# Convolution sums in PSUM, a scan's first group in parts, and transposes in attention

## The chip, the cores and the metric

The kernel runs on one core of a Trainium2 chip, as one launch. The metric is the device time of a launch in microseconds (us); a median over runs is given. The engines are TensorE (PE; its weight loads are listed as PEld), VectorE (DVE), ScalarE (ACT), GpSimd (POOL) and SyncE (SP), whose queue issues the DMAs.

## The reference, cut to what matters

An image batch `x` of 2 x 56 x 56 x 128 passes through four layers, each of them a mixing part and in the last two a feed-forward part:

- Layer 0: a two-dimensional state-space scan (`ss2d`) over 256 inner channels: input projection, depthwise 3x3 convolution with bias and SiLU, four scan directions with 16 states, norm, gate, output projection.
- Layer 1: the same on four heads of 32 channels, one after the other, because each head's input is the sum of its own slice and the output of the head before:

```
for i in range(1, g):
    s = prev + chunks[i]
    prev = _vss_block(s, p) + vss_skip * s      # norm, in_proj, 3x3 conv, SiLU, 4 scans, gate, out_proj
```

- Layer 2: attention of the tokens with themselves as queries, keys and values (one head of 128 channels, 3136 tokens in each of two images), then a spectral mixer (long filters on the token axis).
- Layer 3: attention with projected queries, keys and values, then a mixture of experts.

What is computed by the convolution of one head of layer 1: with both images stacked, 128 channels (64 inner channels x 2 images) of 56 x 56 points, `row = silu(sum over 9 taps of tap * shifted(pad) + bias)`. What is computed by attention for 448 queries: `exp(scale * q.k)` over all keys, the weighted sum of V, and the division by the row sum.

## The kernel before, in words

**Tiling.** A plane of 3136 positions is worked in 7 chunks of 448 columns (`CH`, eight image rows), or in quarters of 784 (`QT`) in the scans, which are 7 tiles of 112 tokens (`TP`, `TS` = 7).

**Layer 1.** `Layer1.run` goes through the heads. It runs the scan of a head (`Scans.run`, some 616 us, an order written out by hand in `emit`), and then a stage between two scans: for each chunk c from 0 to 7, `after` finishes the head just scanned (norm, gate, output projection: L1024 to L1055) and `before` prepares the next head. `before` of chunk c adds the residual (L982), normalises, transposes the tokens to channels (`pt`, L992, copied to `hT`, L994), projects them (L996), writes the result with a border into `pad` (ACT, L997), does the convolution of chunk c - 1 (which needs one row of chunk c), and projects the gate (L1008, L1009). At c == 2 it calls `Scans.first`.

**The convolution** is `conv_rows`. By PE (L522) it is nine matmuls with a diagonal matrix for each tap, in fp32 two passes each, summed in a PSUM tile `pcv`. By DVE it is one TENSOR_SCALAR (L526) and eight SCALAR_TENSOR_TENSOR (L528), summed in place in an SBUF tile `cv`. In heads 1 to 3 the calls c = 2, 4, 5, 6 go to DVE, c = 1, 3, 7 to PE. Then ACT takes the SiLU into `row` (L529; printed as `big`) and POOL copies it into the column order `col` (L530).

**The first group of the next scan** (`Scans.first`) makes what the scan's first sixteen steps read, all at once at c == 2: `rows` (projection, L173, copied by ACT, L185), `keep` (DMA of the rows to DRAM, L189), `fetch` (back, L196), `band` and `rest` (three bf16 bands of each row: ACT L199, POOL L202), `store` (L206), `spread` (the tile `three`, L212), `steps` and `soft` (the step sizes `delta`, L221), `times` (`du`, DVE L231), `across` and `turn` (transposes on PE, L236, copied by ACT, L237). All PSUM tiles of it are `pcv`. In the scan, `spread` (PE, L407) repeats a row of `three` over the partitions into the bank pair `b`, DVE multiplies it by `du` (`h`, L479), scans (L401), POOL multiplies by `c` (L495), and PE adds up (L421).

**PSUM in a stage.** The pools are opened for a stage and closed for the scan, whose own pools take the same banks. Before: `pmid1` with two buffers each of `p`, `pv`, `pt`, and `pcon1` with two buffers of `pcv`.

**Order.** On each engine the order is that of the program; a wait on one engine holds all that is behind it. All DMAs named here are in SP's queue.

**Attention.** `Attend.run` works in 14 chunks (2 images x 7). For each of 25 key tiles PE makes the scores (L1224), ACT the exponentials (L1226), POOL the running row sum `total` (L1237), PE the weighted sum (L1218). At the end of a chunk the sum is copied to SBUF as `by`; four matmuls (L1253) bring it to tokens and apply `out_w`, which for layer 2 is the identity matrix, and four (L1256) sum `total` over the partitions. In layer 3, `Queries.some` prepares the next chunk's queries beside this: low-precision scores (L1159) and their maxima (L1163, L1166); then four matmuls with the identity (L1169) put the 4 x 112 negative maxima into one row in PSUM, ACT copies it to `shift` (L1174), and a bf16 matmul with `part` (L1176) spreads it over the partitions and DVE adds it to `q` (L1177).

Of the kernel before, what the change touches and what calls it, by code (L numbers as in the profile page):

```python
# [14 lines left out]
F32 = mybir.dt.float32  # L15
# [95 lines left out]
class Scans:  # L111
# [138 lines left out]
            soft=soft, copy=copy, times=times, across=across, turn=turn,  # L250
        )

    def first(self, pool):

        self.begin()
        own = {
            "xd": self.y[0][:, 0:QT], "whole": self.y[-1][:, QT : QT + QT // 4],
            "BT": self.y[0][:, QT + QT // 4 : QT + QT // 4 + 32 * TS],
        }
        f = self.pieces_of(self.groups[0], lambda name, n: own[name], self.dram0)  # L260

        def ps():
            return pool.tile([128, CH], F32, name="pcv").unsqueeze(1)

        for i in range(2):
            f["rows"]([i], ps())
        f["keep"]()
        f["fetch"]()
        for i in range(3):
            f["band"](i)  # L270
            if i < 2:
                f["rest"](i)
        f["store"]()
        f["spread"]()
        for ci in range(self.nch):
            for i in range(2):
                f["steps"](ci, [i], ps())
        for ci in range(self.nch):
            f["soft"](ci)
        for ci in range(self.nch):  # L280
            f["times"](ci, False)
        f["across"](ps())
        for ci in range(self.nch):
            for i in range(0, TS, 3):
                f["turn"](ci, ps(), range(i, min(i + 3, TS)))

    def preparation(self, groups, short):

# [219 lines left out]
def conv_rows(k, pools, pad, diag, taps, bias, row, col, c, by):  # L508


    nc = k.nc
    sp, pp = pools
    cs = slice(CH * c, CH * (c + 1))

    def shifted(t):
        dy, dx = divmod(t, 3)
        return pad[:, 8 * c + dy : 8 * c + dy + 8, dx : dx + HW]

    if by == "PE":
        s = pp.tile([128, CH], F32, name="pcv")  # L520
        for t in range(9):
            nc.tensor.matmul(s, lhsT=diag[:, t, :], rhs=shifted(t), start=t == 0, stop=t == 8)  # L522
    else:
        s = sp.tile([128, CH], F32, name="cv")
        v = s.rearrange("p (r w) -> p r w", w=HW)
        nc.vector.tensor_scalar(v, shifted(0), taps[:, 0:1], None, ALU.mult)  # L526
        for t in range(1, 9):
            nc.vector.scalar_tensor_tensor(v, shifted(t), taps[:, t : t + 1], v, ALU.mult, ALU.add)  # L528
# [92 lines left out]
def layer0(k, d, big, follow):  # L621
# [3 lines left out]
    with ExitStack() as ctx:  # L625
# [46 lines left out]
        with ExitStack() as sctx:  # L672
# [117 lines left out]
            for b in range(B):  # L790
                with ExitStack() as bctx:
                    sp = bctx.enter_context(k.pool(f"mid{b}", 2))
                    pp = bctx.enter_context(k.pool(f"pmid{b}", psum=True))
                    cp = bctx.enter_context(k.pool(f"pcon{b}", 2, psum=True))
                    ip = bctx.enter_context(k.pool(f"pads{b}"))
                    if b > 0:
                        outs = outputs(ip)
                    pads = []
                    diag = ip.tile([128, 9, 128], F32, name="diag")
                    for ci in range(2):  # L800
                        pads.append(ip.tile([128, PAD, PAD], F32, name=f"pad{ci}"))
# [12 lines left out]
                    diagonals(k, diag, W["taps"][:, 0])  # L814
                    for c in range(NCH + 1):
                        if b == 0 and c == 2:
                            norm(1, (ap, tp), groups)
                        if b > 0 and c < NCH:
                            after(b - 1, (sp, pp, ip), c, *outs)
                        before(b, (sp, cp), c, pads, diag)  # L820
                        if c == 2:
                            scans.first(cp)
                scans.run()
        with ExitStack() as bctx:
            sp = bctx.enter_context(k.pool("midl", 2))
# [10 lines left out]
class Layer1:  # L836
# [133 lines left out]
    def before(self, head, pools, c, pad):  # L970
# [30 lines left out]
        if c > 0:  # L1001
            conv_rows(
                k, (sp, vp), pad, self.diag, W["taps"], W["conv_b"], self.row, self.col, c - 1,
                "DVE" if c in ((2, 3, 4, 5, 6) if head == 0 else (2, 4, 5, 6)) else "PE",
            )
        if c < NCH:
            ps = vp.tile([128, CH], F32, name="pcv")
            nc.tensor.matmul(ps, lhsT=W["in_w"][:, 1, :], rhs=hT, start=True, stop=True)  # L1008
            nc.scalar.activation(self.z[:, cs], ps, AF.Silu, bias=self.inb[:, 1:2])  # L1009
        if c == 2:  # L1010
            self.scans.first(vp)

    def after(self, head, pools, c):

# [53 lines left out]
    def opened(self, ctx):  # L1068
        k, name = self.k, "mid1"
# [13 lines left out]
    def run(self, follow):  # L1083


        k = self.k
        for head in range(1, 5):
            self.scans.run()
            with ExitStack() as ctx:
                pp = ctx.enter_context(k.pool("pmid1", 2, psum=True))  # L1090
                if head < 4:
                    pad = self.opened(ctx)
                    sp = self.sp
                else:
                    sp = ctx.enter_context(k.pool("mid1", 2))
                    chunk = follow(ctx)
                for c in range(NCH + 1):
                    if c < NCH:
                        self.after(head - 1, (sp, pp), c)
                    if head < 4:  # L1100
                        self.before(head, (sp, pp, self.vp), c, pad)
                    elif c < NCH:
                        self.last(sp, c)
                        chunk(c)
# [18 lines left out]
class Queries:  # L1123
# [27 lines left out]
    def some(self, left):  # L1151
# [12 lines left out]
        if not self.todo:  # L1164
            m = self.sp.tile([TP, 4], F32, name="mm")
            nc.vector.tensor_reduce(m, self.m, AX.X, ALU.max, negate=True)  # L1166
            ps = self.banks("pr")
            for i in range(4):
                nc.tensor.matmul(  # L1169
                    ps[0:1, TP * i : TP * (i + 1)], lhsT=m[:, i : i + 1], rhs=self.k.ident[:TP, :TP],  # L1170
                    start=True, stop=True,
                )
            row = self.sp.tile([1, CH], BF16, name="shift")
            nc.scalar.copy(row, ps[0:1, 0:CH])  # L1174
            ps = self.banks("pr")[:, 0:CH]
            nc.tensor.matmul(ps, lhsT=self.part, rhs=row, start=True, stop=True)  # L1176
            nc.vector.tensor_tensor(self.q, self.q, ps, ALU.add)  # L1177
# [6 lines left out]
class Attend:  # L1184
# [18 lines left out]
    def run(self, keys, queries, V, scale, out_w, skip=None, also=lambda at, j: None):  # L1203
# [4 lines left out]
        for at, (b, qc) in enumerate(chunks):  # L1208
# [41 lines left out]
            pt = four(self.bank("pr"))  # L1250
            pd = av[:TP, CH : CH + 4]
            for i in range(4):
                nc.tensor.matmul(  # L1253
                    pt[:, i, :], lhsT=by[:, TP * i : TP * (i + 1)], rhs=out_w, start=True, stop=True
                )
                nc.tensor.matmul(  # L1256
                    pd[:, i : i + 1], lhsT=total[:, TP * i : TP * (i + 1)], rhs=self.ones, start=True, stop=True
                )
# [7 lines left out]
class Attention2:  # L1266
# [30 lines left out]
    def run(self, early, inputs):  # L1297
# [3 lines left out]
        with k.pool("a2") as sp, ExitStack() as ctx:  # L1301
# [923 lines left out]
```

## Time and profile before

| what | value |
|---|---|
| median of 3 runs | 8746.86 us (8737.68 to 8752.10) |
| profiled execution, its own time | 8761.79 us |
| its span | 8760.0 us |
| mean granted TensorE clock | 0.964 |
| PE, DVE, ACT, POOL busy | 91%, 76%, 64%, 78% |
| scans of layer 1 (start to end, us) | 2768.6 to 3384.7, 3483.9 to 4101.5, 4200.6 to 4814.6, 4912.2 to 5528.4 |
| gaps between them | 99.2, 99.1, 97.6 us |
| a chunk of layer 2's attention | 43.3 us |
| a chunk of layer 3's attention | 54.5 us (early), 49.2 us (later) |

A row of the timeline or of a group reads: start in the span (or the line), busy time, engine, line, operation, output and inputs by the program's names, shapes, and count. In brackets stands how long the engine was idle before and on what it waited. In a windows row, the stretch and its length are followed by the busy time of each engine with its number of instructions, the granted clock of PE as a share of full speed, the share of the DMA engines that was busy, and GB/s. The profiled execution took 14.9 us more than the median of the runs.

### The profile page before, as it was taken

Reading aid. Unit: us, or ns where it says so; the run is one execution under the profiler, and the core shown is the slowest. Engines: PE = TensorE matmul, PEld = TensorE weight load, DVE = VectorE, ACT = ScalarE, POOL = GpSimd, SP = SyncE. Lnnn points to the kernel's source line nnn. Section 1 sums busy time; section 2 is a strip of 40 time slices with the busy share of each in tenths; the row PEclk is TensorE's granted clock in tenths of the full one; section 3 lists DMA queues with packets and bytes.
Section 4 is the critical chain, followed back from the end, with each engine's and each line's share of the span. In section 5 each row is a group of like instructions: output and inputs, shape, how many; then the busy total and the mean of one; then the engine's idle time right before and its main releaser. Section 6 shows DMA issues by size and latency. Waiting matters only on the chain. (4 is left out here: it accounts for less than half of the span.)

```text
span 8760.0 us, 106320 instructions
## 1 busy us (share of the span) xinstructions
PE 8013.3 (91%) x32199; PEld 4929.5 (56%) x32199; DVE 6642.9 (76%) x6889; ACT 5622.6 (64%) x12956; POOL 6845.1 (78%) x4232
## 2 busy tenths in 40 slices
PE   8999999999998898898888889699899989989998
PEld 4555555555555454445444455355488878865555
DVE  8999998999996997998899799711266676665442
ACT  6888876888876997998898799543322222224330
POOL 5999986999995997998899799566667767756551
PEclk9999999999998999999999999799999999989999
DMA  5666663666663884886788598300133433310004
GB/s 147 217 217 210 211 194 115 217 218 214 211 199 96 228 224 127 218 224 165 183 230 219 130 232 223 80 14 4 47 97 102 116 87 101 102 47 8 15 1 140
DMA packets 846633, 1276.86 MB, mean 146 GB/s; under 512 B 182813, under 2 KB 504350, under 8 KB 846058
## 3 DMA queue, kind: packets, MB, share of 16 engines
q1 hardware_dynamic: 846058, 1270.07, 51.8%
q8 instruction: 254, 4.16, 0.2%
q14 instruction: 321, 2.63, 0.1%
HBM read 1230.00 MB, written 46.58 MB: 146 GB/s over the span
## 5 line engine op out<-in xcount | busy, mean ns | idle before, releaser
L495 POOL TENSOR_TENSOR p<-h,c 128x784 f32<-128x784 f32 x2048 | 3765.8, 1867 | 209.2 <-DVE h L401 114.0
L401 DVE TENSOR_TENSOR_SCAN h<-a,state,h 128x784 f32<-128x784 f32 x1104 | 1993.7, 1834 | 29.5 <-POOL h L498 27.2
L421 PE MATMUL acc<-p,center 128*128 128x392 f32 x4096 | 1482.7, 500 | 24.3 <-POOL p L495 24.2
L421 PE MATMUL acc<-p,ident 128*128 128x392 f32 x4096 | 1427.8, 492 | 0.5 <-POOL p L495 0.4
L479 DVE TENSOR_TENSOR h<-du,b 128x784 f32<-128x784 f32 x1024 | 976.9, 954 | 192.5 <-PE b L407 175.5
L421 PEld LDWEIGHTS acc<-p,center 128*128 128x128 f32 x4096 | 747.6, 192 | 546.6 <-POOL p L495 57.2
L421 PEld LDWEIGHTS acc<-p,ident 128*128 128x128 f32 x4096 | 746.5, 190 | 532.4 <-issue 29.5
L1237 POOL TENSOR_TENSOR total<-total,e 128x448 f32<-128x448 f32 (+1 forms) x644 | 735.6, 1142 | 328.7 <-ACT e L1226 289.4
L1226 ACT ACTIVATE e<-sc 128x448 f32<-128x448 f32 (+1 forms) x700 | 377.5, 543 | 723.2 <-PE sc L1224 594.6
L498 POOL TENSOR_TENSOR h<-du,b 128x784 f32<-128x784 f32 x448 | 832.8, 1859 | 0.0
L381 ACT ACTIVATE a<-delta,L1A 128x784 f32<-128x784 f32 x768 | 700.9, 913 | 148.3 <-DVE h L401 144.2
L401 DVE TENSOR_TENSOR_SCAN h<-h,state,a 128x784 f32<-128x784 f32 x432 | 795.4, 1841 | 0.0
L381 ACT ACTIVATE a<-delta,L0A 128x784 f32<-128x784 f32 x704 | 643.0, 914 | 169.8 <-DVE h L401 164.4
L359 ACT ACTIVATE X<-X,BT 112x128 f32<-112x128 f32 x2100 | 683.7, 390 | 0.2
L401 DVE TENSOR_TENSOR_SCAN h<-a,h 128x784 f32<-128x784 f32 x368 | 644.3, 1775 | 29.5 <-POOL h L498 24.0
L1741 POOL TENSOR_TENSOR u<-u,T 128x1024 f32<-128x1024 f32 x192 | 448.9, 2359 | 264.8 <-DVE u L1739 264.8
L407 PE MATMUL b<-three,sel 96*128 96x512 bf16 (+1 forms) x2048 | 516.1, 333 | 100.2 <-DVE h L479 42.7
L1725 ACT ACTIVATE less<-cv 128x512 f32<-128x512 f32 x256 | 152.2, 595 | 611.5 <-PE cv L1703 586.2
L359 ACT ACTIVATE big<-big,BT 112x64 f32<-112x64 f32 x1680 | 446.4, 336 | 0.0
L359 ACT ACTIVATE pair<-big,BT 112x64 f32<-112x64 f32 x1680 | 444.0, 337 | 0.0
L1737 ACT ACTIVATE T<-T 128x1024 f32<-128x1024 f32 x128 | 135.2, 1056 | 407.5 <-DVE T L1735 279.0
L407 PEld LDWEIGHTS <-sel 96*128 96x128 bf16 x2048 | 198.1, 100 | 319.9 <-issue 214.1
(545 smaller groups left out, 15050.5 us busy)
## 6 DMA issues: line engine op xcount, KB each, us to landing
c<-rows SPq DMA_DIRECT2D x1024, 392.0 KB, 4.0
c<-rows SPq DMA_DIRECT2D x2048, 196.0 KB, 4.6
b<-rows SPq DMA_DIRECT2D x512, 196.0 KB, 4.7
b<-rows SPq DMA_DIRECT2D x192, 392.0 KB, 4.5
wA<-win SPq DMA_DIRECT2D x64, 448.0 KB, 3.9
wB<-win SPq DMA_DIRECT2D x64, 448.0 KB, 6.3
wC<-win SPq DMA_DIRECT2D x64, 448.0 KB, 4.8
wD<-win SPq DMA_DIRECT2D x64, 448.0 KB, 3.8
```

Of the source, the lines that this page charges most:

```text
L359: self.k.nc.scalar.activation(x["bT"][:, i, c0:c1], g["duT"][x["ci"]][:, i, c0:c1], AF.Copy, scale=g["BT"][:, r : r + 1])
L381: self.k.nc.scalar.activation(x["a"], g["delta"][ci], AF.Exp, scale=self.w["A"](g["kd"], ci, x["n"]))
L401: self.k.nc.vector.tensor_tensor_scan(h, a, b, start, ALU.mult, ALU.add)
L407: self.k.nc.tensor.matmul(ps[:, c0:c1], lhsT=self.w["selB"](x["n"]), rhs=x["g"]["three"][:, c0:c1], start=True, stop=True)
L421: nc.tensor.matmul(job["acc"][:, i, 0:392], lhsT=self.w["sum"], rhs=x["p"][:, 392 * i : 392 * (i + 1)], start=False, stop=n == NS - 1,)
L479: nc.vector.tensor_tensor(one["h"], one["g"]["du"][one["ci"]], one["b"], ALU.mult)
L495: nc.gpsimd.tensor_tensor(now["p"], now["h"], now["c"], ALU.mult)
L498: nc.gpsimd.tensor_tensor(three["h"], three["g"]["du"][three["ci"]], three["b"], ALU.mult)
L1226: nc.scalar.activation(e[:n], ps[:n], AF.Exp, scale=scale)
L1237: nc.gpsimd.tensor_tensor(total[:n], total[:n], e[:n], ALU.add)
L1725: nc.scalar.activation(turned, self.product(2 * j, pairs), AF.Copy, scale=float(1 + j))
L1741: nc.gpsimd.tensor_tensor(u[:, :, :, o], u[:, :, :, o], half, ALU.add)
```

## The change

It has four parts. In layer 2's attention the four identity matmuls of a chunk become transposes. In layer 3's queries the four identity matmuls of the maxima become one transpose of 112x4 to 4x112, and DVE, in place of ACT, writes them into a 4 x 448 tile in which row i holds tile i's maxima and zeros elsewhere (a product with the identity, broadcast); `part` gets four rows, so that the following matmul adds the rows up. In heads 1 to 3 of layer 1, `conv_rows` has a third way, "PSUM": the DVE instructions, with the sum in a `pcv` tile; calls 1, 3, 5, 6, 7 go that way, and 2 and 4 to PE. And `Scans.first` is divided into parts 2 to 7; heads 1 to 3 call one of them at each chunk from c = 2, where layer 0 and head 0 call all of them in succession. In those heads' stages `pcv` has three buffers and `pt` one, in a pool of its own.

```diff
-    def first(self, pool):
+    def first(self, pool, c):
+        if c == 2:
+            self.begin()
...
+            self.ahead = self.pieces_of(self.groups[0], lambda name, n: own[name], self.dram0)
+        f = self.ahead
...
+        if c == 2:
             for i in range(2):
-                f["steps"](ci, [i], ps())
...
+                f["rows"]([i], ps())
+            f["keep"]()
+        elif c == 3:
+            f["fetch"]()
+            for ci in range(self.nch):
+                for i in range(2):
+                    f["steps"](ci, [i], ps())
+        elif c == 4:
+            for ci in range(self.nch):
+                f["soft"](ci)
+            for i in range(3):
+                f["band"](i)
+                if i < 2:
+                    f["rest"](i)
+            f["store"]()
+            f["spread"]()
+            f["across"](ps())
+        elif c == 5:
+            for ci in range(self.nch):
+                f["times"](ci, False)
+        elif c > 5 and c - 6 < self.nch:
             for i in range(0, TS, 3):
-                f["turn"](ci, ps(), range(i, min(i + 3, TS)))
+                f["turn"](c - 6, ps(), range(i, min(i + 3, TS)))
...
-        s = sp.tile([128, CH], F32, name="cv")
+        s = pp.tile([128, CH], F32, name="pcv") if by == "PSUM" else sp.tile([128, CH], F32, name="cv")
...
-                "DVE" if c in ((2, 3, 4, 5, 6) if head == 0 else (2, 4, 5, 6)) else "PE",
+                ("DVE" if c in (2, 3, 4, 5, 6) else "PE") if head == 0 else "PSUM" if c in (1, 3, 5, 6, 7) else "PE",
...
-        if c == 2:
-            self.scans.first(vp)
+        if c >= 2 and head > 0:
+            self.scans.first(vp, c)
+        elif c == 2:
+            for part in range(2, 8):
+                self.scans.first(vp, part)
...
-        self.vp = ctx.enter_context(k.pool("pcon1", 2, psum=True))
+        self.vp = ctx.enter_context(k.pool("pcon1", n, psum=True))
...
-                    pad = self.opened(ctx)
+                    pad = self.opened(ctx, 3)
+                    qp = ctx.enter_context(k.pool("ptok1", psum=True))
...
-        self.part = sp.tile([1, 128], BF16, name="part")
+        self.part = sp.tile([4, 128], BF16, name="part")
...
-            ps = self.banks("pr")
-            for i in range(4):
-                nc.tensor.matmul(
-                    ps[0:1, TP * i : TP * (i + 1)], lhsT=m[:, i : i + 1], rhs=self.k.ident[:TP, :TP],
-                    start=True, stop=True,
-                )
-            row = self.sp.tile([1, CH], BF16, name="shift")
-            nc.scalar.copy(row, ps[0:1, 0:CH])
+            ps = self.banks("pr")[0:4, 0:TP]
+            nc.tensor.transpose(ps, m, self.k.ident[:TP, :TP])
+            row = self.sp.tile([4, CH], BF16, name="shift")
+            shape = [4, 4, TP]
+            nc.vector.tensor_tensor(
+                row.rearrange("p (i c) -> p i c", c=TP), ps.unsqueeze(1).to_broadcast(shape),
+                self.k.ident[0:4, 0:4].unsqueeze(2).to_broadcast(shape), ALU.mult,
+            )
...
-                nc.tensor.matmul(
-                    pt[:, i, :], lhsT=by[:, TP * i : TP * (i + 1)], rhs=out_w, start=True, stop=True
-                )
+                if out_w is None:
+                    nc.tensor.transpose(pt[:, i, :], by[:, TP * i : TP * (i + 1)], k.ident)
+                else:
+                    nc.tensor.matmul(
+                        pt[:, i, :], lhsT=by[:, TP * i : TP * (i + 1)], rhs=out_w, start=True, stop=True
+                    )
...
-            att.run(self.uT, self.uT, self.V, 128.0**-0.5, k.ident, skip=skip, also=also)
+            att.run(self.uT, self.uT, self.V, 128.0**-0.5, None, skip=skip, also=also)
```

More of the change, by code (lines that the diff above doesn't have):

```diff
@@ L251, in pieces_of @@
         )
-    def first(self, pool):
[L255 to L260, printed above, removed]
+    def first(self, pool, c):
+        if c == 2:
+            self.begin()
+            own = {
+                "xd": self.y[0][:, 0:QT], "whole": self.y[-1][:, QT : QT + QT // 4],
+                "BT": self.y[0][:, QT + QT // 4 : QT + QT // 4 + 32 * TS],
+            }
+            self.ahead = self.pieces_of(self.groups[0], lambda name, n: own[name], self.dram0)
+        f = self.ahead
         def ps():
             return pool.tile([128, CH], F32, name="pcv").unsqueeze(1)
[L265 to L275, printed above, removed]
-            for i in range(2):
-                f["steps"](ci, [i], ps())
[L278 to L283, printed above, removed]
+        if c == 2:
+            for i in range(2):
+                f["rows"]([i], ps())
[19 more added lines that the diff above has]
+        elif c > 5 and c - 6 < self.nch:
             for i in range(0, TS, 3):
-                f["turn"](ci, ps(), range(i, min(i + 3, TS)))
+                f["turn"](c - 6, ps(), range(i, min(i + 3, TS)))
     def preparation(self, groups, short):
@@ L821, in layer0 @@
                         if c == 2:
-                            scans.first(cp)
+                            for part in range(2, 8):
+                                scans.first(cp, part)
                 scans.run()
@@ L1009, in before @@
             nc.scalar.activation(self.z[:, cs], ps, AF.Silu, bias=self.inb[:, 1:2])
-        if c == 2:
-            self.scans.first(vp)
+        if c >= 2 and head > 0:
+            self.scans.first(vp, c)
+        elif c == 2:
+            for part in range(2, 8):
+                self.scans.first(vp, part)
     def after(self, head, pools, c):
@@ L1066, in last, with opened @@
             nc.gpsimd.tensor_tensor(xv, xv, self.R[n].unsqueeze(1).to_broadcast([TP, 4 * B, C]), op)
-    def opened(self, ctx):
-        k, name = self.k, "mid1"
+    def opened(self, ctx, n=2):
+        k = self.k
         self.sp = ctx.enter_context(k.pool("mid1", 2))
-        self.vp = ctx.enter_context(k.pool("pcon1", 2, psum=True))
+        self.vp = ctx.enter_context(k.pool("pcon1", n, psum=True))
         self.ip = ctx.enter_context(k.pool("pad1"))
@@ L1100, in run @@
                     if head < 4:
-                        self.before(head, (sp, pp, self.vp), c, pad)
+                        self.before(head, (sp, qp, self.vp), c, pad)
                     elif c < NCH:
```

## The prediction

> **What bounds the kernel now.** First the busy rows by slice: PE stands near nine tenths in all of the span, but what limits it differs by stage, so the shares are no guide. Then the windows, on the stages that the change touches: the three gaps between scans of the second layer (head 0's scan to head 1's, and so on), one chunk of the second-layer attention (here A2), one early and one later chunk of the third attention (A3), and five microseconds inside the first gap.
>
> ```profile
> core 0: us, PE busy (x) PEld busy (x) DVE busy (x) ACT busy (x) POOL busy (x), PEclk, DMA share, GB/s
> 3384.70:3483.90 99.20, 85.65 (x358) 47.97 (x357) 49.61 (x110) 58.64 (x102) 46.06 (x52) 0.90 0.13 31
> 4101.50:4200.60 99.10, 85.77 (x358) 48.15 (x357) 49.58 (x109) 58.54 (x102) 45.97 (x52) 0.90 0.13 31
> 4814.60:4912.20 97.60, 84.16 (x359) 47.56 (x358) 49.60 (x109) 58.61 (x102) 44.45 (x50) 0.91 0.13 32
> 5759.80:5803.10 43.30, 43.30 (x137) 22.82 (x138) 9.46 (x20) 17.33 (x31) 28.54 (x25) 1.00 0.01 4
> 7971.80:8026.30 54.50, 52.49 (x185) 27.33 (x186) 31.42 (x59) 26.80 (x42) 33.94 (x31) 1.00 0.04 10
> 8128.20:8177.40 49.20, 49.02 (x162) 25.36 (x162) 23.10 (x44) 18.88 (x32) 28.53 (x25) 1.00 0.00 0
> 3445.00:3450.00 5.00, 1.73 (x8) 1.31 (x9) 1.82 (x4) 3.60 (x7) 1.94 (x4) 0.50 0.79 215
> ```
>
> Attention is PE and nothing else: 43.30 of 43.30 us, 49.02 of 49.20. A PE microsecond saved there is a microsecond of the kernel. The gaps are mixed: PE 86% busy, DVE half idle, and PE runs at half clock in the middle. The PE and DVE timelines of the first gap show who ends it:
>
> ```profile
> 3419.21 7.03 PE L522 MATMUL pcv<-pad,diag 128*128 128x448 f32 x18
> ...
> 3452.69 9.63 PE L522 MATMUL pcv<-pad,diag 128*128 128x448 f32 x18
> ...
> 3471.41 1.71 PE L1008 MATMUL pcv<-hT,L1in_w 64*128 64x448 f32 x2 [3.18 <-ACT pair L1009]
> 3473.05 9.69 PE L522 MATMUL pcv<-pad,diag 128*128 128x448 f32 x18
> ```
>
> ```profile
> 3445.74 0.98 DVE L231 TENSOR_TENSOR du<-delta,big 128x784 f32<-128x784 f32 x1 [0.43 <-ACT delta L221]
> ...
> 3453.47 0.45 DVE L526 TENSOR_SCALAR cv<-pad,L1taps 128x448 f32<-128x448 f32 x1 [4.51 <-ACT pad L997]
> ...
> 3464.92 0.69 DVE L528 SCALAR_TENSOR_TENSOR cv<-pad,L1taps,cv 128x448 f32<-128x448 f32 x1 [7.39 <-ACT pad L997]
> ...
> 3471.22 1.20 DVE L526 TENSOR_SCALAR cv<-pad,L1taps 128x448 f32<-128x448 f32 x1
> 3472.34 7.41 DVE L528 SCALAR_TENSOR_TENSOR cv<-pad,L1taps,cv 128x448 f32<-128x448 f32 x10
> 3482.85 0.97 DVE L479 TENSOR_TENSOR h<-du,b 128x784 f32<-128x784 f32 x1 [3.10 <-PE pcv L522]
> ```
>
> Three convolutions run on PE: 7.03 us warm, 9.63 and 9.69 us after a cold start (passes step 0.75 us cold, 0.376 warm). The last stands at the very end: the scan's first multiplication waits 3.10 us for it. DVE waited 4.51 and 7.39 us for `pad` behind the second. And between 3435 and 3451 PE idles six times (2.06, 0.38, 1.10, 0.73, 2.27, 1.50 = 8.0 us), because the next scan's whole first group is queued at c = 2 and each of its steps waits for ACT or DVE.
>
> In attention, the instructions to change:
>
> ```profile
> 5761.31 0.38 PE L1253 MATMUL pr<-ident,by 128*112 128x128 f32 x2
> 5761.53 0.27 PE L1256 MATMUL av<-onecol,total 128*112 128x1 f32 x2
> 5761.65 0.45 PE L1253 MATMUL pr<-ident,by 128*112 128x128 f32 x2
> 8505.54 0.93 PE L1169 MATMUL pr<-ident,mm 112*1 112x112 f32 x8
> 8507.35 0.36 PE L1176 MATMUL pr<-shift,part 1*128 1x448 bf16 x1
> 8506.50 0.52 ACT L1174 CAST shift<-pr 1x448 bf16<-1x448 f32 x1 [0.25 <-PE pr L1169]
> ```
>
> **The base.** All durations are from the profiled execution: span 8760.0, own time 8761.8, 14.9 us above the median of the runs, 8746.9. I sum differences there and take them off the median.
>
> **A2's results by transposes.** An identity matmul in fp32 is two passes; a transpose is one (L236 transposes of the same 128x128 shape step 0.109 us, L992's 112x112 0.095). One L1253/L1256 pair takes 0.415 us, from the starts of successive pairs (between two L1253 starts 0.34 to 0.42). It loses one pass: the second L1253 pass steps 0.110, the first, behind a load of other weights, 0.179. So 0.10 to 0.18 us, four times in a chunk, 14 chunks: 5.8 to 10.0 us, middle **-7.8**. Nothing covers it.
>
> [...] If four transposes let the clock fall, the next passes would run as after 3452.69: 9.63 us against 7.03, so +2.6 us a chunk, +36 us in all. I go by the rows: the clock was 0.50 where PE idled 65% of the time, not by transposing; here transposes are 0.44 us of 43.3, between real passes. I take 0 and keep +36 as a rival.
>
> **A3's shift row.** Eight passes of L1169 (step 0.096, 0.77 us) become one (0.096): 0.67 us saved on PE, 13 to 14 times: 8.7 to 9.4; the first three chunks have 2 us of slack of PE, so **-8.7** (8.0 to 9.4). The ACT copy (0.52) goes; a DVE multiplication of 4x448 from PSUM comes: 0.4 to 0.62 by L1177, PSUM source of the same length. DVE has 26 us idle in 49, and L1176 follows a whole L1224/L1218 later: L1169 ended at 8506.4, L1176 began at 8507.35. It becomes the one to wait if the DVE operation is held by an L1163 reduction (1.16 us for two) in front; slack covers one. Cost 0.
>
> **The gaps, heads 1 to 3.** Head 0 and layer 0 call all parts at once, so their orders stay. In a gap:
>
> - PE loses one convolution of three (18 passes: 7.0 to 9.7 us), the one that ended the stage; the two left (c = 2, 4) fall in a dense stretch. If warm, 14.1 us stand for 26.4.
> - DVE gains one: 9 instructions, 0.45 + 8 x 0.69 = 6.0 us. The order lists put 18 convolution instructions ahead of `du` (9 before) and the same 27 behind it. Ahead: DVE has some 20 us of idle between 3395 and 3446, so the 6 us are covered; without this cover `du`, and with it the tail, would be 6 us later, that is the whole gain.
> - The first group's steps spread over c = 2 to 6: the 8.0 us of PE idle get other chunks' matmuls beside them, so the later `pad`s come earlier.
> - Its DMAs: the row copy goes earlier, `three` (L212) later, behind the b and c loads in SP's queue. It was issued at 3454.6 and first read at 3466.7: 12 us of slack against landings of 4.0 to 4.7 us for such loads. If every hop of the chain landed in 4.5 us instead of some 2, the first group would be 4 to 5 us later and the gain down to 2 us.
> - POOL's two band subtractions (L202) move behind the skips and L530 copies of two more chunks; POOL is busy 46 of 99 us and the 12 us of slack hold for them too.
> - The third bank for `pcv` is paid by `pt`, now single. The first spread (L407) uses banks of `pcv`, so it now waits for ACT's L529 of the second-last convolution; behind it on PE stand only more spreads. The last convolution on DVE waits for a buffer that `turn`'s copy (L237) frees; behind it stands `h`, for which the scan waits.
>
> Sum on DVE, from the gap's start: `du` ends at 62.0 as now. Then it waits for `pad` through PE's convolution of c = 4, warm: 6.2 (now 11.9 in two waits). Then 27 instructions: 19.2 now, of which one L526 was 1.20 beside POOL's L530 instead of 0.45: 18.4. Reductions and roots between, 2.3. Buffer wait 0 to 3.6 (an L237 series; take 1.8). L529 and the cold L407 before `h`: 1.3. Together 92.0; `h` starts at 98.15 now. So **-6** a gap, -18 for three. Bounds: no buffer wait and a warm PE, -8; the DMA hops slow or the DVE cover gone, 0.
>
> The price of a SCALAR_TENSOR_TENSOR whose running sum is in PSUM is in no row of before (DVE never writes PSUM there). Nearest rows: L479, a PSUM source of 784, 954 ns; L231, both sources SBUF, 950 to 976; so equal. [...] Below nothing: the DVE instruction would no longer have two SBUF inputs, and those beside POOL's L530 took 0.92 to 1.24 us instead of 0.69; that can give 1 us a gap.
>
> **Total**: -7.8 - 8.7 - 18 = -34.5: span 8725.5, median **8712**. The scans themselves (616 us each) have the same instructions and I leave them.
>
> **The rivals.**
>
> - *The gaps give nothing* (chance 0.20). The wait only changes its name: for PE's convolution now, for a `pcv` buffer, L529 with its 1.28 us table load, or the spread's bank then. For: DVE gets the longer tail and ACT sits in it (58.6 of 99 busy). Against: PE's 9.69 us at the end are truly gone. Attention alone: -16.5, **8730**.
> - *The transposes save little* (0.10): weight loads set the pace, since PEld takes 0.13 us for each. Against: L236 does it at 0.109. Attention -6, gaps -18: **8723**.
> - *Slower: DVE's sums in PSUM cost double* (0.05), each reading and writing one bank. Place: the 27 in the tail. At 1.37 us for 0.69: +18.4 - 6 = +12.4 a gap, +37, less 16.5: +21, **8768**. The gap breaks even at 6/27 = 0.22 us more for each, the kernel at 34.5/81 = 0.43, and it is slower by 0.2% from 0.64. Against: the PSUM-source rows above.
> - *Transposes cool PE's clock* (0.03): +36 in place of -7.8: +9, **8756**.
> - That the change doesn't do what it says is so for head 0 only: three gaps, not four; counted.
>
> **How the numbers follow.** The forecast has 0.62: 8712, by its bounds 8700 (-8 and -1 a gap, -19.4 in attention) to 8728. About 0.2%, 17.5 us, is what a measurement of this kernel can tell from no change; the line is at 8729.4. The forecast and the second rival are faster (0.72); the first lies on the line, 0.09 faster and 0.11 same; cooling is same (0.03), double price slower (0.05). So 0.81, 0.14, 0.05. The range holds the forecast and the first rival, and on each side 7 us, half of the spread of the runs before: 8693 to 8737.
>
> **What would show it.** A2's chunk at 42.6 to 42.9 us with the clock at 1.00; A3's at 48.6; the gaps at 91 to 94 us with `h` behind DVE's own sums or L407, and no PE convolution in the last 20 us; PE idle in the middle down from 8 us. SCALAR_TENSOR_TENSOR into `pcv` at 0.62 to 0.75. I am wrong if these cost 0.9 or more, if gaps stay at 98 with a wait for L529 or L237 at the end, or if a scan's length moves.

## The result, and the profile after

Over 11 runs of each the changed kernel takes 8718.76 us in the median (8704.09 to 8731.50), the kernel before 8746.86. The ratio is 0.9966, 95% interval [0.9958, 0.9974]: 23 to 37 us faster. Forecast were 8712 and -34.5; the measured difference of the medians is -28.1.

The profiled execution of the changed kernel took 8719.8 us (span 8718.0), near its median, while that of before lay 14.9 above its own. So the two profiles differ by 42 us where the runs differ by 28; the difference has to be read stage by stage. First the windows of the stages that changed, in the same columns as before (PE, PEld, DVE, ACT, POOL busy; granted PE clock; DMA): three gaps between second-layer scans, a chunk of A2, an early and a later chunk of A3.

```profile
3379.70:3471.30 91.60, 75.15 (x341) 42.78 (x340) 54.24 (x119) 61.15 (x104) 44.02 (x51) 0.88 0.13 33
4082.90:4174.50 91.60, 75.20 (x341) 42.80 (x340) 54.27 (x119) 61.16 (x104) 44.03 (x51) 0.88 0.13 34
4789.80:4881.30 91.50, 75.38 (x341) 42.84 (x340) 54.22 (x118) 61.07 (x104) 43.92 (x51) 0.88 0.13 34
5725.60:5768.20 42.60, 42.60 (x133) 22.07 (x133) 9.43 (x19) 17.33 (x31) 28.53 (x25) 1.00 0.01 4
7919.50:7973.10 53.60, 51.31 (x178) 26.72 (x177) 32.32 (x59) 26.16 (x41) 34.02 (x31) 1.00 0.03 10
8082.50:8130.80 48.30, 48.12 (x155) 24.82 (x156) 23.71 (x46) 18.36 (x31) 28.53 (x25) 1.00 0.00 1
```

The gaps go from 99.2, 99.1 and 97.6 us to 91.5 each (rounded from 91.54, 91.51 and 91.52): -21.3 together. PE is 9 to 11 us less busy in each, DVE 4.6 us more. A2's chunk went from 43.2 to 42.6 (13 chunk-to-chunk distances sum to 561.6 before and 554.2 after), A3's from 49.2 to 48.3 (645.9 and 635.1). PE still has next to no pause in both (42.60 of 42.60 us and 48.12 of 48.30 busy), and the full clock (1.00). Lines moved by 6 in the scans (L401 is L407, L407 is L413) and by 6 to 14 elsewhere.

PE and DVE in the first gap after:

```profile
3418.36 7.03 PE L528 MATMUL pcv<-pad,diag 128*128 128x448 f32 x18
...
3438.67 7.03 PE L528 MATMUL pcv<-pad,diag 128*128 128x448 f32 x18
...
3469.34 0.81 PE L413 MATMUL b<-three,sel 96*128 96x512 bf16 x2 [7.98 <-ACT big L535]
```

```profile
3440.84 0.98 DVE L231 TENSOR_TENSOR du<-delta,big 128x784 f32<-128x784 f32 x1
...
3448.21 0.69 DVE L532 TENSOR_SCALAR pcv<-pad,L1taps 128x448 f32<-128x448 f32 x1 [2.05 <-ACT pair L1016]
...
3461.43 0.69 DVE L532 TENSOR_SCALAR pcv<-pad,L1taps 128x448 f32<-128x448 f32 x1 [3.53 <-ACT big L237]
3462.03 7.72 DVE L534 SCALAR_TENSOR_TENSOR pcv<-pad,L1taps,pcv 128x448 f32<-128x448 f32 x12
3470.19 0.97 DVE L485 TENSOR_TENSOR h<-du,b 128x784 f32<-128x784 f32 x1 [0.44 <-PE b L413]
```

Both PE convolutions now run warm, 7.03 us each (by the trace's record the clock is 1.00 from 3357.8 to 3450.0), and none stands at the end. What ends the stage is DVE: `h` starts 0.44 us after its last sum. Of the new waits, the one for a `pcv` buffer (3.53 us, until turn's copy L237) is real; PE's 7.98 us before the first spread cost nothing but that 0.44, since DVE is still summing. PE's pauses in the middle have shrunk less than was hoped: 0.70 and 0.91 us before its second convolution and six from 3447 to 3460, 4.5 us together, where there were 8.0 before. From 3450.0 on its clock is 0.50; what that costs here was not measured.

And a stage that nothing in the change touches: the experts' router, some 20 us after the end of A3, which sums 28 token tiles with small matmuls, each with weights of its own. PE's rows of the second of its groups, before and then after:

```profile
8593.98 3.70 PE L1996 MATMUL ps<-shares,sel 128*112 128x128 f32 x16
8597.47 4.14 PE L2004 MATMUL sum<-selT,X 112*128 112x64 f32 x32
```

```profile
8540.89 3.70 PE L2010 MATMUL ps<-shares,sel 128*112 128x128 f32 x16
8544.38 6.93 PE L2018 MATMUL sum<-selT,X 112*128 112x64 f32 x32
```

The windows of the same stretch, two of before and then two of after, tell why:

```profile
8591.00:8596.00 5.00, 5.00 (x25) 5.00 (x26) 0.00 (x0) 0.00 (x0) 0.00 (x0) 0.50 0.00 0
...
8601.00:8606.00 5.00, 5.00 (x46) 4.89 (x46) 1.38 (x2) 0.00 (x0) 0.00 (x0) 1.00 0.00 0
```

```profile
8543.00:8548.00 5.00, 5.00 (x26) 5.00 (x24) 1.30 (x2) 0.00 (x0) 0.00 (x0) 0.50 0.00 0
...
8558.00:8563.00 5.00, 5.00 (x25) 4.99 (x24) 0.00 (x0) 0.00 (x0) 0.00 (x0) 0.50 0.00 0
```

In these windows PE is busy all the time in both, but in the changed kernel the clock stays at 0.50 to the end of the router: 37.6 us from its first to its last matmul, 27.5 before. From A3's last chunk to the end of the launch it is 11.1 us more (196.8 and 207.8).

So the profiles' 42 us: gaps -21.3, A2 and A3 -18.2, router and what follows +11.1, the four second-layer scans -9.5 (2464.0 and 2454.5 us), the rest of the launch -4, which was not traced. The scans have the same instructions; among the five profiles of kernels whose layers up to the scans are those of the changed kernel they took from 2454.5 to 2474.8, so -9.5 lies within their scatter. Without them and the rest it is -28.4, near the -28.1 of the runs. That is agreement and not proof: the router is seen only in profiled launches, one for each kernel.

### The profile page after: what moved, and what is told of

It reads as the page before. It is cut to its first block, busy times and chain, and to the rows that moved or that the text cites. A ratio compares the mean times of both kernels' runs of the same rounds, so it can differ in the third digit from the quotient of the medians.

```text
span 8718.0 us, 105946 instructions
## 1 busy us (share of the span) xinstructions
PE 7962.1 (91%) x31991; PEld 4900.5 (56%) x31991; DVE 6666.9 (76%) x6930; ACT 5620.3 (64%) x12948; POOL 6842.5 (78%) x4232
## 5 line engine op out<-in xcount | busy, mean ns | idle before, releaser
L407 DVE TENSOR_TENSOR_SCAN h<-a,state,h 128x784 f32<-128x784 f32 x1104 | 1993.3, 1834 | 26.6 <-POOL h L504 24.0
L407 DVE TENSOR_TENSOR_SCAN h<-h,state,a 128x784 f32<-128x784 f32 x432 | 795.4, 1841 | 0.0
L407 DVE TENSOR_TENSOR_SCAN h<-a,h 128x784 f32<-128x784 f32 x368 | 644.1, 1774 | 25.7 <-POOL h L504 20.5
L413 PE MATMUL b<-three,sel 96*128 96x512 bf16 (+1 forms) x2048 | 516.4, 333 | 124.7 <-DVE h L485 42.5
L413 PEld LDWEIGHTS <-sel 96*128 96x128 bf16 x2048 | 197.7, 100 | 341.2 <-issue 234.5
```

The costliest lines, as they stand in the source:

```text
L407: self.k.nc.vector.tensor_tensor_scan(h, a, b, start, ALU.mult, ALU.add)
L413: self.k.nc.tensor.matmul(ps[:, c0:c1], lhsT=self.w["selB"](x["n"]), rhs=x["g"]["three"][:, c0:c1], start=True, stop=True)
```

## The experiments

Medians of the kernel before differ between the groups of runs (8746 to 8756 us), so ratios are used, each from 5 to 11 runs of the kernel; one launch of each was profiled. "Router" is the time from the first to the last matmul of the router's sums in the profile.

**The attention edits alone**, in the kernel before.

> The kernel before with the two attention edits alone (A2's transposes, the shift row). If the parts add up: A2's chunk 42.7 us as in the changed kernel (43.3 before), A3's 48.3 (49.2), together -20 us (8.0 and some 12), the gaps 99 us as before, so ratio 0.9977. If the attention gain is partly eaten by the experts' router, which in the profile of the changed kernel ran at half clock for 25 us longer and took 11 us more, and if that comes from the attention edits, then the router is slow here too and the time is -9 to -10 us. If the router's clock is a draw of each launch, independent of the change, the profiles of these experiments show it fast in some and slow in others, also without attention edits.

Measured: ratio 0.9993 [0.9984, 1.0002], -6 us. A2's and A3's distances are those of the changed kernel (554.2, 635.1), the gaps 99.2, 99.5, 99.2; the router took 37.6 us. So the chunks gain their 18 us, and in the profile the router gives 10 of it back. The runs fit that, but their interval, -14 to +2 us, is wide.

**The gaps alone**: the changed kernel with attention as before.

> The changed kernel with attention as before: the second layer's gaps alone. If the parts add up: gaps 91.5 us three times, attention chunks 43.3 and 49.2, time -21 to -23 us, ratio 0.9975. If the router's slowness follows from the attention edits, it is fast here, and always; if it is a draw, either.

Measured: 0.9983 [0.9974, 0.9991], -15 us; gaps 91.5 three times, router 22.6 us. The gaps are as expected (-21); the runs' interval, -8 to -23 us, holds that, their middle is below it. With the 5 us that this profile's router took less than that of before, -26 would be due, outside the interval; more on this below.

**Sums in SBUF**, everything else as changed:

```
-        s = pp.tile([128, CH], F32, name="pcv") if by == "PSUM" else sp.tile([128, CH], F32, name="cv")
+        s = sp.tile([128, CH], F32, name="cv")
```

> The changed kernel, but the five DVE convolutions of a gap sum in an SBUF tile again (the third PSUM buffer stays). Theory 1, the gap's gain comes from the order and from PE's third convolution, not from PSUM as such: DVE's waits of 3.5 us for a PSUM buffer before the last convolution and PE's wait for the SiLU of the one before fall away, the one-input instruction is 0.45 us instead of 0.69, so the gap is 85 to 90 us, below 91.5. Theory 2, PSUM pays because a sum in SBUF is held up by POOL (single instructions up to 1.9 us in the profile before): the SCALAR_TENSOR_TENSORs average 0.71 to 0.75 instead of 0.68, and the gap is above 91.5, 92 to 96 us.

Measured: 0.9971 [0.9960, 0.9983]; gaps 92.0, 88.9, 92.2, mean 91.1. Neither theory: the wait for a buffer is gone, but sums are held up. The group in the first gap (busy us, mean ns):

```profile
L534 DVE SCALAR_TENSOR_TENSOR cv<-pad,L1taps,cv 128x448 f32<-128x448 f32 x40 | 28.5, 736 | 0.9 <-ACT pad L1004 0.3
```

736 ns against 682 in PSUM, with one instruction of 2.12 us; `du` ends 1.2 us later. All 20 of this profile's 160 second-layer sums that took over 0.8 us lie beside an instruction of POOL; of the 120 in PSUM none took over 0.69. PSUM as such is worth at most half a microsecond a gap here, and the runs tell no difference from the changed kernel; what counts is who sums, and when. What the third `pcv` buffer is worth by itself was not tested.

**The first group all at once** at c = 2 in all heads, the rest as changed.

> The changed kernel with the first group of the next scan prepared all at once at c = 2, as before, in all heads; convolutions and banks as changed. If the parts of the group fill PE's idle time, as the prediction said, this kernel loses 4 to 6 us of a gap's 7.6: gaps 95 to 98 us, PE idle some 8 us in the middle again, total -24 to -28 against the first kernel with attention's 20. If the convolutions alone carry the gap, they stay at 91 to 93 us.

Measured: 0.9979 [0.9970, 0.9988]; gaps 96.9, 96.8, 96.9. The division into parts is worth 5.4 of a gap's 7.1 to 7.6 us. PE idles in the middle again, in these rows of its timeline:

```profile
3433.14 0.26 PE L999 MATMUL pt<-ident,nrm 112*64 112x112 f32 x1 [3.29 <-ACT hT L1001]
...
3436.40 1.86 PE L1003 MATMUL pcv<-hT,L1in_w 64*128 64x448 f32 x2 [1.09 <-ACT big L237]
...
3456.44 1.86 PE L1015 MATMUL pcv<-hT,L1in_w 64*128 64x448 f32 x2 [2.58 <-ACT pad L1004]
```

**Three convolutions on PE as before** (c = 1, 3, 7), the parts as changed:

```
-                ... "PSUM" if c in (1, 3, 5, 6, 7) else "PE",
+                ... "PSUM" if c in (2, 4, 5, 6) else "PE",
```

> The changed kernel, but with the convolutions divided as before: PE takes c = 1, 3, 7 in heads 1 to 3, DVE (sums in PSUM) 2, 4, 5, 6; first group in parts, banks as changed. Theory 1, the convolution taken from PE's end is needed for the gap: PE ends the stage again with c = 7's matmuls, gaps 98 to 103 us, so the parts alone bring nothing. Rival, the parts alone carry the gap: 93 to 95 us. Total against the changed kernel +18 to +30 us by theory 1.

Measured: 0.9988 [0.9979, 0.9997]; gaps 101.3, 101.2, 101.1. Theory 1 holds: PE ends the stage again, with a convolution of 9.35 us as after the cold starts of before (9.63 and 9.69; warm 7.03), and the parts without the move are 2 us worse than the kernel before. PE's timeline at the end of the gap:

```profile
3465.14 9.35 PE L528 MATMUL pcv<-pad,diag 128*128 128x448 f32 x18 [0.35 <-ACT big L237]
3475.90 0.49 PE L413 MATMUL b<-three,sel 96*128 96x512 bf16 x2 [1.41 <-ACT big L535]
```

The two edits need each other. Its router, with A3 as changed, took 22.7 us.

**Turn's pieces in the bank of `pt`**:

```
+            if other is not None and c > 5:
+                return other.tile([128, CH], F32, name="pt").unsqueeze(1)
             return pool.tile([128, CH], F32, name="pcv").unsqueeze(1)
```

> The changed kernel with the three transposed pieces of `du` (turn) in the bank of `pt` and not in `pcv`. In the changed kernel DVE waits 3.5 us before the last convolution for a `pcv` buffer that turn's copy frees. If this wait is what ends the stage now, gaps are 88 to 89 us instead of 91.5, total -8 to -10 us. If another wait stands behind it (the SiLU before the first spread), the gaps stay at 91 us.

Measured: 0.9956 [0.9941, 0.9972]; gaps 90.1, 89.7, 89.8. The runs don't tell it apart from the changed kernel. Half of the wait comes back as others, each for ACT or for the spread; DVE's timeline (lines moved by 2):

```profile
3450.50 0.69 DVE L534 TENSOR_SCALAR pcv<-pad,L1taps 128x448 f32<-128x448 f32 x1 [0.71 <-ACT pair L1018]
...
3456.10 0.69 DVE L534 TENSOR_SCALAR pcv<-pad,L1taps 128x448 f32<-128x448 f32 x1 [1.36 <-ACT pair L1018]
3456.70 8.18 DVE L536 SCALAR_TENSOR_TENSOR pcv<-pad,L1taps,pcv 128x448 f32<-128x448 f32 x13
3465.91 0.97 DVE L487 TENSOR_TENSOR h<-du,b 128x784 f32<-128x784 f32 x1 [1.04 <-PE b L415]
```

**Matmuls ahead of the router**, in the changed kernel:

```
+                for i in range(5):
+                    nc.tensor.matmul(
+                        gp.tile([128, CH], F32, name="warm"), lhsT=k.ident, rhs=pr[:, 0:CH], start=True, stop=True
+                    )
```

> The changed kernel with five extra fp32 matmuls (128x448, result unused) in PE's 7.1 us of idle time before the experts' router sums. If the router's 37.6 us (27.5 in the profile of before, 22.6 in that of the gaps alone) are PE's clock and nothing else, it takes 20 to 23 us here with the clock at 1.00, and the launch is 10 to 17 us faster than the changed kernel. Rival: the clock falls again in this stream of small matmuls, because each waits for its weights, and nothing changes.

Measured: 0.9959 [0.9945, 0.9973], against 0.9966 [0.9958, 0.9974] of the changed kernel: by the runs not told apart. The profile's router took 22.4 us, and the stretch from A3's last chunk to the end 188.8 us (207.8). The matmuls ran in a pause of PE ahead of the last gates, 6.8 us long, not in the one of 7.1 us right before the sums.

**The shift row as before**, the rest as changed.

> The changed kernel with the third attention's shift row as before (four fp32 matmuls, ACT's copy): A3's chunk back at 49.2 us. Plain sum: +12 us against the changed kernel. If the shift row is what leaves the router cold (all four profiles of kernels with both attention edits show it at 37.6 us, both of kernels without them faster), the router takes 22 to 28 us here and the total is -3 to +2 against the changed kernel. If the router is a draw of each launch that the edits don't touch, +12 in the median.

Measured: 0.9972 [0.9963, 0.9981]; A3's distances 645.8, router 27.6 us, so in the profile A3's -10.8 and 10 of the router cancel, as the second theory has it; the runs (+5 us on the changed kernel's ratio, give or take 10) do not separate this from the plain sum. Its first gap took 100.6 us, the others 91.5, in this one launch, and the clock is lower there. Windows of that gap:

```profile
3407.00:3412.00 5.00, 4.30 (x18) 2.44 (x19) 2.59 (x7) 1.10 (x2) 4.57 (x7) 0.73 0.00 0
3412.00:3417.00 5.00, 5.00 (x17) 3.08 (x16) 2.87 (x8) 3.95 (x6) 2.91 (x4) 0.50 0.01 2
...
3422.00:3427.00 5.00, 5.00 (x13) 2.66 (x13) 0.00 (x0) 2.55 (x3) 0.00 (x0) 0.50 0.00 0
```

By the trace's record the clock fell to half at 3409.3 and stayed there for 20.5 us, in which PE was busy throughout; the gap is 9 us longer. PE's longest pause in the 25 us before was 0.99 us, ended at 3407.7. The same pause, 0.99 us ahead of the same transposes, stands in the first gaps of the kernel before and of the changed kernel, where the clock stayed full; so the pause alone doesn't do it, and the cause stays open.

**1.5 us of work added in the middle of A3**, in the changed kernel (two fp32 matmuls of 128x448), to move all that follows:

> The changed kernel with two extra fp32 matmuls of 128x448 (1.5 us of PE, result unused) in the middle of A3's sixth chunk. Clock changes fall on a grid of 3.41 us, and the third attention keeps PE's place on this grid: in the nine profiles without extra matmuls at the router the half-clock stretch begins 14.6 to 14.8 us before the router's sums (or 3.41 more) where it lasts 58 to 61 us, 15.5 to 15.6 before where it lasts 31, 15.7 to 16.0 where it lasts 20. Theory: the shift row made A3 some 11 us shorter, and that moved the router to the bad place of the grid. Then 1.5 us more work moves it to about -16.3, the router takes 22.6 to 27.6 us and not 37.6, and the launch is 8 to 13 us faster than the changed kernel in spite of the added work. Rival, the edit itself (transposes, less PE work ahead) cools the router: 37.6 us again, and the launch is 1.5 us slower.

Measured: 0.9960 [0.9947, 0.9974]; A3's distances 636.6, the half-clock stretch began 16.0 us before the router's sums and lasted 20.5, router 22.6 us, from A3's last chunk to the end 190.2 us. The profile, one launch, is as the theory says: 1.5 us more work and 17.6 us less behind it. The runs' middle is 5 us faster than the changed kernel's; they don't tell the two apart.

**2.6 us of work added in A3 of the kernel before**:

> The kernel before with 2.6 us of extra fp32 matmuls (three of 128x448, one of 128x224, results unused) in the middle of A3's sixth chunk: nothing of the change. Before, the half-clock stretch began 15.6 us before the router's sums. By the theory of the grid the router moves to about -18.2, one period from -14.8, and takes 37.6 us with the clock at 0.50 throughout; the launch is 13 to 18 us slower than before, of which 2.6 are the matmuls. By the rival (the edit of the shift row cools it) the router stays at 22 to 28 us and the launch is 2.6 us slower.

Measured: 1.0012 [1.0003, 1.0021], +10 us; but the profiled launch had its stretch at -15.2 us, and the router took 27.7. In that launch A3 itself began 0.4 us later on the grid than in the profile of before (the stretch ahead of it 83.9 and not 83.5 us earlier), and -18.2 became -15.2, that is -18.6 and one period. The place was missed, so this launch didn't test what it was made for: it is neither for the theory nor against it, and the runs' interval, 2.6 to 18 us, allows both.

**Turn's pieces and the matmuls together**, in the changed kernel.

> The changed kernel with the two additions together: turn's pieces in the bank of `pt` (gaps 89.8 us for 91.5 when alone), and five fp32 matmuls ahead of the router's sums (router 22.4 us for 37.6 when alone). If both hold: gaps 89.8, router 22.5, 5 us and 15 us less than the profile of the changed kernel, total 8698 to 8706 in the median, ratio to before 0.994 to 0.995. If the router's gain is made up elsewhere: as with turn's pieces alone.

Measured: 8705.95 us in the median, ratio 0.9943 [0.9931, 0.9956]: 38 to 60 us faster than the kernel before, and just clear of the changed kernel's interval (0.9956 against 0.9958). Gaps 89.7 three times, router 22.3 us. PE's timeline:

```profile
8517.42 6.66 PE L1997 MATMUL warm<-pr,ident 128*128 128x448 f32 x10
...
8533.85 3.75 PE L2016 MATMUL ps<-shares,sel 128*112 128x128 f32 x16 [7.11 <-DVE shares L2007]
8537.66 3.79 PE L2024 MATMUL sum<-selT,X 112*128 112x64 f32 x32
```

The first sixteen passes took 3.75 us, near the 3.70 that the changed kernel's took at a clock of 0.50; the sixteen of the next group (from 8541.28) took 1.95. It is faster than both kernels.

**The attention edits with the matmuls**, in the kernel before: the first experiment, without its loss.

> The two attention edits alone, as in the first experiment, with the five fp32 matmuls ahead of the router's sums. Alone the edits moved the launch by a ratio of 0.9993 only, where their chunks say -19 us (0.9978). If the rest was given back in the router at half clock (37.6 us), it takes 22.4 us here, and the ratio is 0.9965 to 0.9978 (-19 to -30 us). If it was lost elsewhere, or the first experiment's runs were only slow by chance in other places, the ratio stays near 0.999.

Measured: 0.9979 [0.9970, 0.9988], -18 us where the edits alone gave -6; router 22.3 us, A2 and A3 554.1 and 635.0. By the medians most of attention's gain, some 19 us, is there when the router is warm. The two intervals overlap by a hair, 0.9984 and 0.9988 being their nearer ends, so this is likely and not certain.

**What the router's clock hangs on.** In the trace's record of the granted clock all stretches at 0.50 but the last of a launch, which its end cuts off, last a multiple of 3.41 us (79 of 80 in the profile of before, 68 of 69 in that of the changed kernel); call the places where they can begin and end the grid. Eleven profiles, all but those with matmuls ahead of the router:

| stretch begins before the router's sums | it lasts | router | kernels |
|---|---|---|---|
| 14.6 to 14.8 us, or 18.2 (3.41 more) | 58.0, 61.4 us | 37.6 us | changed; attention alone; sums in SBUF; group at once; turn |
| 15.2 | 30.7 | 27.7 | before with 2.6 us |
| 15.5, 15.6 | 30.7 | 27.5 | before; shift row as before |
| 15.7 to 16.0 | 20.5 | 22.6, 22.7 | gaps alone; three convolutions; changed with 1.5 us |

The place on the grid tells the router's time in every one of them. But the rows were set up when nine of the profiles were known; of the two launches made to test them, the one with 1.5 us more hit and the one with 2.6 missed its place. So the grid is well supported, and not proven. A3, in which PE has next to no pause (48.12 of 48.30 us of a chunk busy), carries its place through: its first chunk ended 83.0 to 83.9 us after the start of such a stretch in all of these, and its length is what differs, by 10.8 us, which is three periods and 0.6 us. The three-convolution kernel has the edited A3, but there it took 1 us longer, and it is in the last row. So the shift row's edit as such does not cool the router; it makes A3 end at another place. That A3's start keeps so near to one place in launches of different lengths was seen and not explained.

It also bears on the kernel before: its profiled launch, 15 us above the median, may not be typical. An estimate from the numbers above, with -21 us for the gaps, -19 for attention (14 chunks of 0.57 and 12 of 0.92) and each profile's router: if the router of most launches of before took 22.6 us, as in the gaps alone, and not 27.5, the sums would be -4 for the attention edits (runs: -6), -21 for the gaps (-15), -19 for attention with the matmuls (-18), -24 for the shift row as before (-24) and -25 for the change (-28). With 27.5 each comes out 5 us lower, and the gaps alone fall outside their interval. No run here decides it.

## Why the prediction was right, step by step

- **A2**: forecast -7.8, -0.56 a chunk; measured -0.57 (43.2 to 42.6), -8.0 for 14. The four pairs of a chunk took 1.59 us from the first start to the next key's matmul (5761.31 to 5762.90) and take 1.02 (5727.10 to 5728.12). By the starts of its rows a pair takes 0.23 to 0.27 us instead of 0.34 to 0.42:

```profile
5727.10 0.27 PE L1265 MATMUL pr<-ident,by 128*112 128x128 f32 x1
5727.21 0.27 PE L1270 MATMUL av<-onecol,total 128*112 128x1 f32 x2
5727.33 0.30 PE L1265 MATMUL pr<-ident,by 128*112 128x128 f32 x1
```

Four transposes in a chunk had no visible effect on the clock: it is 1.00 in the chunk's window (5725.60 to 5768.20), with PE busy for 42.60 of 42.60 us. The rival of cooling transposes, whose +36 us was an estimate from the cold convolution, is out, at that place.

- **A3**: forecast -8.7 from 0.67 us a row; measured 0.92 in a steady chunk, -10.8 over 13 distances (the last chunk prepares no queries). The term was mis-sized: I counted the eight passes at their own step (0.77 us) and left out that the steps are longer where weights and shape change: 0.469 us from the key's last pass into the row (0.376 between passes of that shape), 0.190 from its last pass to the next matmul (0.096). From the start of the key's matmul before the row to the start of the next it was 1.71 us (8504.69 to 8506.40), and is 0.87 (8162.69 to 8163.56); without a row between them it is 0.75 to 0.76. So the row cost 0.96 and costs 0.12. The remaining 0.09 comes at the `part` matmul, counted in the same way: 1.23 and 1.14. Before, then after:

```profile
8504.69 0.92 PE L1224 MATMUL sc<-q,u 128*128 128x448 f32 x2
...
8506.40 1.02 PE L1218 MATMUL av<-e,V 128*128 128x448 f32 x2
```

```profile
8162.69 0.92 PE L1235 MATMUL sc<-q,first 128*128 128x448 f32 x2
8163.47 0.26 PE L1179 MATMUL pr<-ident,mm 112*4 112x112 f32 x1
8163.56 0.93 PE L1229 MATMUL av<-e,first 128*128 128x448 f32 x2
8164.32 0.91 PE L1235 MATMUL sc<-q,first 128*128 128x448 f32 x2
8165.17 0.36 PE L1187 MATMUL pr<-shift,part 4*128 4x448 bf16 x1
```

DVE's product took 0.61 us (top of its bounds) and was done 0.8 us before L1187.

- **The gaps**: forecast -18, measured -21.3. By the terms of the sum on DVE: `du` ends at 62.1 us (62.0); the first tail instruction starts 6.4 us later (6.2), right in size but not by the wait that was named: DVE stands 3.35 us for ACT's L83 and then 2.05 for L1016, which frees a `pcv` buffer, and not for `pad` (PE's convolution of c = 4 stands ahead of L1016 too, so the path is half right); the 27 instructions take 17.7 us (18.4); the buffer wait 3.5 (1.8, bound 3.6); the reductions (2.3) fall into the first wait; 0.3 goes to one more wait for L1016; from the last sum to `h` 0.4 instead of 1.3, because the spread waits for the second-last SiLU only, which ends 0.5 us before the last sum does. `h` starts at 90.5 (92.0).
- **DVE's sums in PSUM** cost what I took. The rows of all heads, min/median/max in ns, after and before:

```profile
L534 DVE SCALAR_TENSOR_TENSOR pcv<-pad,L1taps,pcv x120: 636/682/691, 3412.4 to 4879.1; 128x448 f32<-128x448 f32 x120
L532 DVE TENSOR_SCALAR pcv<-pad,L1taps x15: 671/686/687, 3411.7 to 4871.5; 128x448 f32<-128x448 f32 x15
```

```profile
L528 DVE SCALAR_TENSOR_TENSOR cv<-pad,L1taps,cv x136: 653/685/1877, 2675.8 to 4909.1; 128x448 f32<-128x448 f32 x136
...
L526 DVE TENSOR_SCALAR cv<-pad,L1taps x17: 441/453/1206, 2675.3 to 4901.2; 128x448 f32<-128x448 f32 x17
```

682 against 685: these rows show no extra for a sum that is read from PSUM and written there, and the rival of double price is out. What I did not price: the one-input instruction goes from 453 to 686 ns, +0.23 us, five times a gap. In return no sum in PSUM is above 0.69 us, where in SBUF single ones reach 1.88.
- **Not in the sum at all**: the router, in the profiles +10 to +11 us. I had looked for the clock's answer inside the attention chunks and not behind them.
- The total came within 6 us partly by luck: the gaps and A3 gave 5 to 6 us more than forecast, and the router, which was not thought of, took 11.

## What to carry to other kernels

Taking an engine's work from a stage's end pays in full only if the work ahead of it flows: here the move alone or the division alone gave 2 or -2 us a gap, and both 7. The gains in the two stages that PE fills came there (-8.0 us in A2, -10.8 in A3), but by the profiles they can shift what follows on the clock's grid (router 37.6 us for 27.5): read the clock and PE's row in the next stage of small matmuls before booking a gain, and if that stage runs cold, try matmuls in a pause ahead of it (here 22.4 us for 37.6 in the profile). When changing a few small matmuls between large ones, count from the start of the neighbour before to the start of the neighbour after, not the passes alone.

## What of the hardware was not expected

- PE can be busy without a pause, by the profile's records, and stay at half clock: in the router of the changed kernel from 8538 to 8563, 25.00 of 25.00 us, in a stretch of 58.0, and in a gap 20.5 of 20.5, where the longest pause ahead was 1 us. The stretches at half clock are multiples of 3.41 us, but for the last of each launch, and 25 us of full work, over seven times 3.41, did not lift the clock.
- Much of the scatter between runs goes with that clock: in 28 runs of the kernel before, from 8728 to 8765 us, a straight line through time and mean clock (given to 0.001) falls by 5.4 us for each 0.001, with a correlation of -0.87. A mean lower by 0.001 is 17.5 us of the span at half clock, worth at most 9 us if all of it were PE's work: an estimate from the span of 8760 us and the trace's record of the clock, which holds 1.00 and 0.50 alone.
- A TENSOR_SCALAR in fp32 that writes PSUM took 0.686 us for 448 columns instead of 0.453 into SBUF; a SCALAR_TENSOR_TENSOR took the same in both (0.682 and 0.685).
